# Every third image through the two-row form in both parts, in a convolution kernel with group normalisation

## The chip, the cores and the metric

One core of one Trainium2 chip. The metric is the device time of one execution in microseconds (us), the median of several runs. Each kernel was timed beside runs of the kernel before on the same chip.

Engines: PE is TensorE (PEld its weight loads), DVE is VectorE, ACT is the scalar engine, POOL is GpSimd, SP issues DMA. The timelines show the instructions of each of DVE, ACT and POOL in the order in which this program issues them (DVE of run e14 below has 30 in a row in that order, from 555.94 to 575.24 us).

## The reference, cut to what matters

```python
# x: (160, 128, 32, 32) fp32;  U: (5, 128*128*3*3)
v  = group_norm(x, 32 groups, eps=1e-5)       # over 4 channels x 32 x 32
s1 = (max(U) - min(U)) / 3;  v1 = s1 * floor(U / s1)
s2 = s1 / 5;                 v2 = s2 * floor((U - v1) / s2)
w  = (v1 + v2)                                # five sets of 3x3 weights, 128 -> 128
out = x + conv3x3(v, w[set of the image], pad=1)
```

Images are worked through set by set, 32 to a set. The weights of the next set are quantised while the present set is convolved.

## The kernel before: the parts that matter

fp16 matmuls are made accurate by splitting each normalised image z in two: `hi` (z in fp16) and `lo` (the rest). `hi` is convolved with all nine taps. `lo` goes through a **two-row form**: a pair of output rows is made from row differences `d` and from sums and differences `st` of row pairs, with combined weights, which needs fewer columns on PE. A sum `m` and the rest `eo` gather in PSUM, where PE's results lie until an engine fetches them; ACT moves `m` out, DVE forms the two rows of each pair and adds everything, and a DMA that accumulates adds the result to x in SBUF, from where it is stored.

```python
def conv(self, i, on_the_way):              # PE, image i
    ...                                     # m: 2 kinds x 3 columns, 512 wide, from st
    eo = ...
    for col in self.COLS:
        self.taps(i, (self.hi[i], 0), col, eo, False)     # 6 matmuls, 512 wide: hi, 3 taps x 2 halves
        ...                                               # 4 matmuls, 256 wide, from d
def leave(self, i):                         # ACT: m out of PSUM
def pairs(self, i):                         # DVE: two rows from each pair of m
def residual(self, i):                      # DVE: sum tile = pairs + eo; frees the PSUM tile eo
    self.sum[i] = self.sums.tile(...)       # pool "sums": 3 buffers
def accumulate(self, i):                    # POOL: DMA adds the sum tile to x
def store(self, i):                         # SP: store of a chunk of NB = 4 images

for i in range(self.imgs):                  # one round (cut)
    self.conv(i, on_the_way)
    self.normalise(i + 3)                   # ACT: z
    ...                                     # ACT: sum over image i + 13, if not by DVE
    self.leave(i)
    self.high_part(i + 3)                   # ACT: hi
    self.low_part(i + 2); self.combinations(i + 2)   # DVE
    self.residual(i - 1); self.pairs(i)              # DVE
    ...                                     # ACT: sum of squares; POOL: group means, deviations
    take(later, 2)                          # DVE: two steps of the next set's weights
    self.accumulate(i - 1); self.store(i - 2); ...   # loads
```

## Time and profile before

| | before |
|---|---|
| time | 1084.4 us (1083.8 to 1085.2) |
| busy | PE 97%, DVE 82%, ACT 71%, POOL 36% of 1082.9 us |
| chain that ended last | PE 94% |
| PE, one convolution | 6.42 us, 157 of them |

A line of groups reads: source line, engine, operation, result from operands, shape, count; then total busy us and mean ns of one; then the engine's idle time just before, and what ended most of it. In the timeline, a bracket holds the idle time before an instruction and what it waited for. The lines themselves are in the prediction below.

### The profile page before, as it was taken

The page shows a single profiled execution, that of the slowest core. Times are in us where ns is not written, and L with a number is a line of the kernel's source. Part 1 is how long each engine was busy: PE and PEld are TensorE (multiplying, and loading weights), DVE is VectorE, ACT ScalarE, POOL GpSimd, SP SyncE. Part 2 cuts the span into 40 slices and gives each one's busy share as a digit, 9 for nine tenths or more (in the row PEclk, how much of TensorE's full clock was granted, in tenths as well). Part 3 has the DMA queues.
Part 4 walks back from the last instruction along what each step waited for, and adds up shares of the span by engine and source line. Part 5 has one row for each costly group of instructions (what it writes and reads, how often), then busy time and mean ns, then how long its engine had stood idle before and what let it go on. Part 6 is the DMA issues. An engine that isn't in the chain of part 4 may idle for free.

```text
span 1082.9 us, 16003 instructions
## 1 busy us (share of the span) xinstructions
PE 1045.6 (97%) x5910; PEld 576.3 (53%) x5910; DVE 889.1 (82%) x1471; ACT 773.2 (71%) x1041; POOL 391.8 (36%) x738
## 2 busy tenths in 40 slices
PE   1899999999999999999999999999999999999997
PEld 0355555555555555555555555555555555555554
DVE  7998998877898988778898968798988777776774
ACT  4788886777768777767686877687777777677541
POOL 4634535332425343324435332334353313232210
PEclk9999999999999999999999999999999999999999
DMA  9518898989798889998897989798989898985764
GB/s 362 213 20 243 241 266 240 262 243 251 231 251 231 259 233 255 247 261 221 245 246 221 252 233 276 202 254 257 258 233 254 238 274 213 266 212 149 173 165 159
DMA packets 65462, 252.05 MB, mean 233 GB/s; under 512 B 3936, under 2 KB 3936, under 8 KB 65376
## 3 DMA queue, kind: packets, MB, share of 16 engines
q1 hardware_dynamic: 43344, 170.73, 42.2%
q0 software_dynamic: 22032, 80.23, 39.9%
q8 instruction: 48, 0.79, 0.3%
q14 instruction: 38, 0.31, 0.1%
HBM read 86.84 MB, written 83.89 MB: 158 GB/s over the span
## 4 chain that ended last, share of the span: by engine, by line
PE 94%; DVE 3%; ACT 1%; DMA 1%; issue 0%; POOL 0%; SPq 0%; DVEq 0%
PE eo L515 55%; PE eo L545 19%; PE m L545 19%; DMA u<-in_L_conv_U_dram 1%; PE m L515 1%; DVE ext L391 0%; DVE ext L392 0%; ACT z L468 0%; PE pt L428 0%; DVE tt L109 0%; PE pg L219 0%; DVE lo L481 0%; PE pg L204 0%; DVE k L113 0%; DVE tt L111 0%
## 5 line engine op out<-in xcount | busy, mean ns | idle before, releaser
L515 PE MATMUL eo<-hi,wt 128*128 128x512 f16 (+1 forms) x2862 | 684.7, 376 | 0.6 <-ACT wt L433 0.6
L515 PEld LDWEIGHTS <-wt 128*128 128x128 f16 x2934 | 287.7, 99 | 273.2 <-issue 2.3
L545 PEld LDWEIGHTS <-wt 128*128 128x128 f16 x2826 | 276.1, 98 | 194.9 <-issue 1.0
L545 PE MATMUL eo<-d,wt 128*128 128x256 f16 (+1 forms) x1884 | 283.3, 273 | 0.0
L573 ACT ACTIVATE mm<-m 128x1024 f16<-128x1024 f32 x157 | 159.8, 1018 | 158.0 <-PE m L545 157.9
L545 PE MATMUL m<-st,wt 128*128 128x512 f16 x942 | 229.3, 380 | 0.8 <-ACT mm L573 0.8
L468 ACT ACTIVATE z<-xt,shift,rstd 128x1024 f32<-128x1024 f32 x160 | 197.5, 1234 | 44.4 <-POOL shift L235 44.3
L481 DVE TENSOR_TENSOR lo<-z,hi 128x1024 f16<-128x1024 f32 x160 | 194.9, 1218 | 8.9 <-ACT hi L476 8.9
L602 DVE SCALAR_TENSOR_TENSOR sum<-pq,eo 128x1024 f32<-128x1024 f16 x153 | 185.5, 1213 | 17.5 <-PE eo L545 17.5
L582 DVE TENSOR_TENSOR pq<-mm 128x512 f16<-128x512 f16 x157 | 66.2, 422 | 135.2 <-ACT mm L573 134.0
L198 POOL TENSOR_SCALAR mv<-squares 128x1 f32<-128x1 f32 x121 | 63.5, 525 | 305.3 <-ACT junk L195 303.6
L615 POOL DMA_DIRECT2D xt<-sum x153 | 136.0, 891 | 85.3 <-DVE sum L602 69.5
L476 ACT CAST hi<-z 128x1024 f16<-128x1024 f32 x160 | 166.0, 1037 | 0.1
L195 ACT ACTIVATE junk<-xt,minus 128x1024 f16<-128x1024 f32 x121 | 139.1, 1150 | 2.6 <-POOL minus L188 1.4
L186 ACT ACTIVATE junk<-xt 128x1024 f16<-128x1024 f32 x121 | 126.4, 1045 | 12.1 <-DMA xt<-in_x_dram 11.9
L495 DVE TENSOR_TENSOR d<-lo 128x1024 f16<-128x1024 f16 x157 | 108.9, 694 | 5.4
L188 POOL TENSOR_SCALAR minus<-total 128x1 f32<-128x1 f32 x121 | 39.9, 329 | 97.2 <-ACT junk L186 96.5
L498 DVE TENSOR_TENSOR st<-lo 128x512 f16<-128x512 f16 x157 | 66.4, 423 | 0.0
L497 DVE TENSOR_TENSOR st<-lo 128x512 f16<-128x512 f16 x157 | 65.8, 419 | 0.0
L583 DVE TENSOR_TENSOR pq<-mm 128x512 f16<-128x512 f16 x157 | 65.4, 417 | 0.0
L179 DVE BATCH_NORM_STATS2 st<-xt 128x6 f32<-128x512 f32 x78 | 49.8, 679 | 0.0
L214 POOL TENSOR_TENSOR dv<-mv,ngm 128x8 f32<-128x8 f32 (+2 forms) x23 | 11.7, 509 | 89.6 <-ACT ngm L212 86.7
(96 smaller groups left out, 445.3 us busy)
## 6 DMA issues: line engine op xcount, KB each, us to landing
xt<-in_x_dram SPq DMA_DIRECT2D x39, 2048.0 KB, 14.0
out_dram<-xt SPq DMA_DIRECT2D x39, 2048.0 KB, 7.3
xt<-sum POOLq DMA_DIRECT2D x153, 512.0 KB, 8.2
u<-in_L_conv_U_dram SPq DMA_DIRECT2D x4, 576.0 KB, 8.1
xt<-in_x_dram SPq DMA_DIRECT2D x4, 512.0 KB, 10.5
out_dram<-xt SPq DMA_DIRECT2D x3, 512.0 KB, 3.1
u<-in_L_conv_U_dram SPq DMA_DIRECT2D x2, 288.0 KB, 3.0
out_dram<-xt SPq DMA_DIRECT2D x2, 256.0 KB, 3.5
```

The lines of the kernel that those rows point to most:

```text
L186: nc.scalar.activation(junk, image, ACTF.Copy, accum_out=total)
L195: nc.scalar.activation(junk, image, ACTF.Square, bias=self.minus[j], accum_out=squares)
L468: nc.scalar.activation(z, self.image(i), ACTF.Identity, bias=st.shift[:, j : j + 1], scale=st.rstd[:, j : j + 1],)
L476: self.nc.scalar.copy(hi.rearrange("p h w -> p (h w)"), self.z[i])
L481: self.nc.vector.tensor_sub(lo[:, 1 : self.H + 1, :].rearrange("p h w -> p (h w)"), self.z.pop(i), self.hi[i].rearrange("p h w -> p (h w)"),)
L495: nc.vector.tensor_sub(d, lo[:, 0:H, :], lo[:, 2 : H + 2, :])
L498: nc.vector.tensor_sub(st[:, 1], pairs[:, 1], pairs[:, 0])
L515: nc.tensor.matmul(target[:, h, r0 - h0 : r1 - h0, c0:c1], self.wts[n, col][:, k, :], tile[:, s0 : s0 + r1 - r0, c0 + dw : c1 + dw], start ...
L545: nc.tensor.matmul(target[:, :, c0:c1], self.wts[n, col][:, kind, :], source[:, :, c0 + dw : c1 + dw], start=start, stop=stop,)
L573: self.nc.scalar.mul(m, self.m.pop(i).rearrange("p a i w -> p a (i w)"), UP)
L602: nc.vector.scalar_tensor_tensor(self.sum[i], self.m.pop(i), 0.5 / UP, eo, ALU.mult, ALU.add)
L615: self.nc.gpsimd.dma_start(self.image(i), self.sum.pop(i), accum_op=ALU.add)
```

## The change

Every third image from image 14 on (48 of them) goes through the two-row form in **both** parts. For such an image DVE combines rows of x in fp32 (`v`), ACT rounds the combination to fp16 (`vh`), DVE makes the remainder (`vl`), and PE multiplies both. PE is rid of 18 wide taps, and runs the two-row form twice. Beside that, chunks become two images (11 buffers for 6 larger ones), all statistics from image 14 on move to ACT and are made one image earlier, and weights of later sets are loaded again when wanted. For the image after a combined one PE starts with `hi` and multiplies its `m` one column later (not in the cut below). A limit that guards the fast path is tightened for accuracy.

```diff
-NB = 4
+NB = 2
-LEAST, MOST = 2.0**-10, 0.06
+LEAST, MOST = 2.0**-10, 0.04
-    STAT_LEAD = 13
+    STAT_LEAD = 14
+    STEADY = 14
-        self.xpool = pool("x", 6)
+        self.xpool = pool("x", 11)
...
-        return i >= self.EARLY and (i % 4 == 0 or i == 10)
+        return self.EARLY <= i < self.STEADY and (i % 4 == 0 or i == 10)
...
+    def combined(self, i):
+        return self.STEADY <= i < self.imgs - LAST and i % 3 == 2
+    def combine(self, i):
+        v = self.v[i] = self.wide.tile([P, 2048], F32, tag="v", name=f"v{i}")
+        nc.gpsimd.tensor_scalar(v[:, :W], x[:, W : 2 * W], minus, -1.0, ALU.add, ALU.mult)
+        nc.gpsimd.tensor_scalar(v[:, last : H * W], ...)        # first and last row
+        nc.vector.tensor_sub(v[:, W:last], x[:, : last - W], x[:, 2 * W :])
+        nc.vector.scalar_tensor_tensor(s, pairs[:, 0], st.twice[:, j], pairs[:, 1], ALU.add, ALU.add)
+        nc.vector.tensor_sub(t, pairs[:, 1], pairs[:, 0])
+    def high_combined(self, i):
+        self.nc.scalar.mul(vh, self.v[i], st.rstd[:, j])
+    def low_combined(self, i):
+        self.nc.vector.scalar_tensor_tensor(vl, self.v[i], st.rstd[:, j], self.hi[i], ALU.mult, ALU.subtract)
...
     def pairs(self, i):
+        if self.combined(i):
+            pq = self.sums.tile([self.P, 1024], F32, tag="sum", name=f"sum{i}")
...
     def residual(self, i):
+        if self.combined(i):
+            nc.vector.tensor_add(self.sum[i], eo, self.sum[i])
...  # in the round of image i
+            if self.combined(i + 1):
+                self.low_combined(i + 1)
+            if self.combined(i + 2):
+                self.combine(i + 2)
...
+            if self.combined(i + 2):
+                self.high_combined(i + 2)
```

More of the change, by code (lines that the diff above doesn't have):

```diff
@@ L21 @@
 EPS = 1e-5
-NB = 4
+NB = 2
+LAST = 4
 LIFT = 2.0**14
-LEAST, MOST = 2.0**-10, 0.06
+LEAST, MOST = 2.0**-10, 0.04
 UP = 32.0
@@ L235, in scales @@
         nc.gpsimd.tensor_tensor(self.shift, self.ngm, self.rstd, ALU.mult)
+        self.twice = self.tile("twice", [self.nb])
+        nc.gpsimd.tensor_scalar_mul(self.twice, self.ngm, 2.0)
 def general_path(tc, keep, steps, x, u, out):
@@ L343, in __init__ @@
         self.wpool = pool("weights", 2)
-        self.xpool = pool("x", 6)
+        self.upool = pool("u", 1)
+        self.xpool = pool("x", 11)
         self.zpool = pool("z", 3)
-        self.parts = pool("parts", 5)
+        self.parts = pool("parts", 4)
         self.rows = pool("rows", 4)
+        self.wide = pool("wide", 1)
+        self.wide_parts = pool("wide_parts", 2)
         self.evac = pool("evac", 2)
@@ L369, in place, with space, load_set @@
         return divmod(i, self.per_set)
+    def space(self, name):
+        return self.xpool.tile([self.P, NB, 1024], F32, tag="xt", name=name)
+    def load_set(self, n):
+        self.us[n] = self.upool.tile([self.P, self.P, TAPS], F32, tag="u", name=f"u{n}")
+        self.nc.sync.dma_start(self.us[n], self.uv[n])
     def load(self, c, single=False):
-        xt = self.xpool.tile([self.P, NB, 1024], F32, tag="xt", name=f"xt{c}")
+        xt = self.space(f"xt{c}")
         self.chunks[c] = xt
@@ L477, in high_part, with column_of @@
         self.hi[i] = hi
+    def combined(self, i):
+        return self.STEADY <= i < self.imgs - LAST and i % 3 == 2
+    def column_of(self, i):
+        k = self.group_of[i]
+        j = i - self.groups[k].start
+        return self.stats[k], slice(j, j + 1)
+    def combine(self, i):
+        nc, P, H, W = self.nc, self.P, self.H, self.W
+        st, j = self.column_of(i)
+        v = self.v[i] = self.wide.tile([P, 2048], F32, tag="v", name=f"v{i}")
+        x = self.image(i)
+        minus, last = st.ngm[:, j], (H - 1) * W
+        nc.gpsimd.tensor_scalar(v[:, :W], x[:, W : 2 * W], minus, -1.0, ALU.add, ALU.mult)
+        nc.gpsimd.tensor_scalar(
+            v[:, last : H * W], x[:, last - W : last], minus, 1.0, ALU.add, ALU.mult
+        )
+        nc.vector.tensor_sub(v[:, W:last], x[:, : last - W], x[:, 2 * W :])
+        pairs = x.rearrange("p (i a w) -> p a i w", a=2, w=W)
+        s, t = (v[:, k : k + 512].rearrange("p (i w) -> p i w", w=W) for k in (1024, 1536))
+        nc.vector.scalar_tensor_tensor(
+            s, pairs[:, 0], st.twice[:, j], pairs[:, 1], ALU.add, ALU.add
+        )
+        nc.vector.tensor_sub(t, pairs[:, 1], pairs[:, 0])
+    def high_combined(self, i):
+        st, j = self.column_of(i)
+        vh = self.wide_parts.tile([self.P, 2048], MM, tag="vh", name=f"vh{i}")
+        self.nc.scalar.mul(vh, self.v[i], st.rstd[:, j])
+        self.hi[i] = vh
+    def low_combined(self, i):
+        st, j = self.column_of(i)
+        vl = self.rows.tile([self.P, 2048], MM, tag="rows", name=f"vl{i}")
+        self.nc.vector.scalar_tensor_tensor(
+            vl, self.v[i], st.rstd[:, j], self.hi[i], ALU.mult, ALU.subtract
+        )
+        self.v[i] = vl
     def low_part(self, i):
@@ L492, in combinations @@
         lo = self.los[i % len(self.los)]
-        d = self.rows.tile([P, H, W], MM, tag="d", name=f"d{i}")
-        st = self.rows.tile([P, 2, H // 2, W], MM, tag="st", name=f"st_{i}")
+        d, st = self.halves(self.rows.tile([P, 2048], MM, tag="rows", name=f"rows{i}"))
         nc.vector.tensor_sub(d, lo[:, 0:H, :], lo[:, 2 : H + 2, :])
@@ L499, in combinations, with halves @@
         self.v[i] = (d, st)
+    def halves(self, v):
+        return (
+            v[:, :1024].rearrange("p (h w) -> p h w", w=self.W),
+            v[:, 1024:].rearrange("p (a i w) -> p a i w", a=2, w=self.W),
+        )
     def taps(self, i, part, col, target, last):
@@ L539, in conv @@
         n, _ = self.place(i)
-        d, st = self.v.pop(i)
+        combined = self.combined(i)
+        if combined:
+            both = [self.halves(v) for v in (self.hi[i], self.v.pop(i))]
+        else:
+            both = [self.v.pop(i)]
+        late = self.combined(i - 1)
         def product(target, kind, source, col, start, stop):
@@ L551, in product, with sums_of_pairs @@
             )
-        m = self.m[i] = self.banks(self.ps_m, "m", i)
-        for a, kind in enumerate((self.SUM, self.DIFF)):
-            for col in self.COLS:
-                product(
-                    m[:, a], kind, st[:, a], col, col == self.COLS[0], col == self.COLS[-1]
-                )
+        def sums_of_pairs():
+            m = self.m[i] = self.banks(self.ps_m, "m", i)
+            for a, kind in enumerate((self.SUM, self.DIFF)):
+                for col in self.COLS:
+                    for _, st in both:
+                        product(
+                            m[:, a], kind, st[:, a], col,
+                            col == self.COLS[0] and st is both[0][1],
+                            col == self.COLS[-1] and st is both[-1][1],
+                        )
@@ L559, in conv @@
+        if not late:
+            sums_of_pairs()
         eo = self.eo[i] = self.banks(self.ps_eo, "eo", i)
         for col in self.COLS:
+            if late and col == self.COLS[1]:
+                sums_of_pairs()
             if col == self.COLS[-1]:
                 on_the_way()
-            self.taps(i, (self.hi[i], 0), col, eo, False)
+            if not combined:
+                self.taps(i, (self.hi[i], 0), col, eo, False)
             for a, kind in enumerate((0, self.MINUS_G2)):
-                for h in range(2):
-                    rows = slice(h * 16 + a, h * 16 + 16, 2)
-                    to = eo[:, h].rearrange("p (i a) w -> p i a w", a=2)[:, :, a, :]
-                    product(to, kind, d[:, rows, :], col, False, col == self.COLS[-1] and a == 1)
@@ L570, in leave @@
-    def leave(self, i):
-        m = self.evac.tile([self.P, 2, 512], MM, tag="mm", name=f"mm{i}")
-        self.nc.scalar.mul(m, self.m.pop(i).rearrange("p a i w -> p a (i w)"), UP)
+                for d, _ in both:
+                    for h in range(2):
+                        rows = slice(h * 16 + a, h * 16 + 16, 2)
+                        to = eo[:, h].rearrange("p (i a) w -> p i a w", a=2)[:, :, a, :]
+                        product(
+                            to, kind, d[:, rows, :], col,
+                            combined and col == self.COLS[0] and a == 0 and d is both[0][0],
+                            col == self.COLS[-1] and a == 1 and d is both[-1][0],
+                        )
@@ L574, in leave @@
+    def leave(self, i):
+        if self.combined(i):
+            m = self.wide.tile([self.P, 2, 512], F32, tag="m", name=f"mw{i}")
+            scale = 0.5
+        else:
+            m = self.evac.tile([self.P, 2, 512], MM, tag="mm", name=f"mm{i}")
+            scale = UP
+        self.nc.scalar.mul(m, self.m.pop(i).rearrange("p a i w -> p a (i w)"), scale)
         self.m[i] = m
@@ L579, in pairs @@
         m = self.m.pop(i).rearrange("p a (i w) -> p a i w", w=self.W)
-        pq = self.evac.tile([self.P, 1024], MM, tag="pq", name=f"pq{i}")
+        if self.combined(i):
+            pq = self.sums.tile([self.P, 1024], F32, tag="sum", name=f"sum{i}")
+        else:
+            pq = self.evac.tile([self.P, 1024], MM, tag="pq", name=f"pq{i}")
         rows = pq.rearrange("p (i a w) -> p i a w", a=2, w=self.W)
@@ L590, in by_hand @@
     def by_hand(self, i):
-        return i < self.FIRST or i >= self.imgs - NB
+        return i < self.FIRST or i >= self.imgs - LAST
     def residual(self, i):
@@ L599, in residual @@
         n, b = self.place(i)
+        if self.combined(i):
+            self.sum[i] = self.m.pop(i)
+            nc.vector.tensor_add(self.sum[i], eo, self.sum[i])
+            return
         if not self.by_hand(i):
@@ L609, in residual @@
             nc.vector.tensor_add(xj[:, h], eo[:, h], xj[:, h])
-            if i >= self.imgs - NB:
+            if i >= self.imgs - LAST:
                 nc.sync.dma_start(self.ov[n, :, b, h], xj[:, h])
@@ L617, in store @@
     def store(self, i):
-        if 0 <= i < self.imgs - NB and i % NB == NB - 1:
+        if 0 <= i < self.imgs - LAST and i % NB == NB - 1:
             n, b = self.place(i)
@@ L625, in run @@
         nc, P = self.nc, self.P
-        self.us = []
+        self.us = {}
         for n in range(N_SETS):
-            un = self.const.tile([P, P, TAPS], F32, tag=f"u{n}", name=f"u{n}")
+            if n == 0:
+                un = self.upool.tile([P, P, TAPS], F32, tag="u", name="u0")
+            else:
+                un = self.space(f"range{n}").rearrange("p j e -> p (j e)")[:, : P * TAPS]
+                un = un.rearrange("p (i k) -> p i k", k=TAPS)
             half = P // 2 if n == 0 else P
@@ L631, in run @@
                 nc.sync.dma_start(un[:, c : c + half], self.uv[n][:, c : c + half])
-            self.us.append(un)
-        self.load(0, single=True)
-        self.load(1)
-        self.load(2)
+            self.us[n] = un
+        for c in range(6):
+            self.load(c, single=c < 2)
         warm = self.const.tile([P, 1], F32, tag="warm", name="warm")
@@ L656, in run @@
         nc.vector.memset(self.ones, 1.0)
-        spread = self.over_partitions(self.weight_range(self.us), ident)
+        spread = self.over_partitions(self.weight_range(list(self.us.values())), ident)
         def take(steps, count):
@@ L731, in run @@
         self.steps.choose()
-        ready, middle, measured, loaded, later = [], [], self.EARLY, 3, None
+        ready, middle, measured, loaded, later = [], [], self.EARLY, 6, None
         for i in range(self.imgs):
@@ L758, in run @@
             measured += len(to_measure)
-            if self.FIRST < i + 3 < self.imgs:
-                self.normalise(i + 3)
+            parted = [
+                k for k in (i + 3, i + 4)
+                if self.FIRST < k < self.imgs and not self.combined(k)
+                and k - 3 - self.combined(k - 1) == i
+            ]
+            if self.combined(i + 1):
+                self.low_combined(i + 1)
+            if self.combined(i + 2):
+                self.combine(i + 2)
+            for k in parted:
+                self.normalise(k)
             for k in to_measure:
@@ L765, in run @@
                 self.leave(i)
-            if self.FIRST < i + 3 < self.imgs:
-                self.high_part(i + 3)
-            if self.FIRST < i + 2 < self.imgs:
-                self.low_part(i + 2)
-                self.combinations(i + 2)
+            for k in parted:
+                self.high_part(k)
+            if self.combined(i + 2):
+                self.high_combined(i + 2)
+            if i + 2 < self.STEADY:
+                if self.FIRST < i + 2:
+                    self.low_part(i + 2)
+                    self.combinations(i + 2)
             if i > self.FIRST:
@@ L774, in run @@
                 self.pairs(i)
+            if self.STEADY <= i + 2 < self.imgs and not self.combined(i + 2):
+                self.low_part(i + 2)
+                self.combinations(i + 2)
             for st in middle:
@@ L785, in run @@
                     ready.append(self.stats[group])
+            if b == self.per_set // 16 and n + 1 < N_SETS:
+                self.load_set(n + 1)
             if b == self.per_set // 8 and n + 1 < N_SETS:
```

## The prediction

> **What bounds the kernel now.** I read the page's totals and the chain that ended last first, then one image in the timeline, then the groups by form, then the waits, then DMA in slices of 1 us. Totals, clock and chain:
>
> ```profile
> PE 1045.6 (97%) x5910; PEld 576.3 (53%) x5910; DVE 889.1 (82%) x1471; ACT 773.2 (71%) x1041; POOL 391.8 (36%) x738
> ...
> PEclk9999999999999999999999999999999999999999
> ...
> PE 94%; DVE 3%; ACT 1%; DMA 1%; issue 0%; POOL 0%; SPq 0%; DVEq 0%
> ```
>
> The reader sees PE busy throughout, at full clock, and 94% of the chain is PE. The waits agree: PE's largest, 18.9 us, is one in the start-up, and in the 157 convolutions that follow it waits for others about 1 us. So this is a PE-bound kernel: the time is the start-up (the first such convolution starts near 66.7 us), 157 convolutions, and a short tail. What matters is what one convolution costs on PE. The timeline around 507 us, PE only:
>
> ```profile
> 506.91 1.46 PE L545 MATMUL m<-st,wt 128*128 128x512 f16 x6
> ...
> 508.21 1.43 PE L515 MATMUL eo<-hi,wt 128*128 128x512 f16 x6
> ...
> 509.48 0.60 PE L545 MATMUL eo<-d,wt 128*128 128x256 f16 x4
> 509.92 1.43 PE L515 MATMUL eo<-hi,wt 128*128 128x496 f16 x6
> ...
> 513.33 1.46 PE L545 MATMUL m<-st,wt 128*128 128x512 f16 x6
> ```
>
> Durations overlap (pipelined), so I take differences of starts: m to the next m is 6.42 us for 36 matmuls. Six 512-wide ones take 508.21-506.91 = 1.30 us (217 ns each), four 256-wide ones 509.92-509.48 = 0.44 us (110 ns each). A row of 31 costs like one of 32. Check: 6 + 18 x (full or 480) + 12 x 256 is 15,168 columns; at 2.4 per ns plus 36 x 2.5 ns that is 6.41 us.
>
> The other engines have room, but not much. The groups I use below:
>
> ```profile
> L468 ACT ACTIVATE z<-xt,shift,rstd 128x1024 f32<-128x1024 f32 x160 | 197.5, 1234 | 44.4 <-POOL shift L235 44.3
> L481 DVE TENSOR_TENSOR lo<-z,hi 128x1024 f16<-128x1024 f32 x160 | 194.9, 1218 | 8.9 <-ACT hi L476 8.9
> L602 DVE SCALAR_TENSOR_TENSOR sum<-pq,eo 128x1024 f32<-128x1024 f16 x153 | 185.5, 1213 | 17.5 <-PE eo L545 17.5
> L476 ACT CAST hi<-z 128x1024 f16<-128x1024 f32 x160 | 166.0, 1037 | 0.1
> L573 ACT ACTIVATE mm<-m 128x1024 f16<-128x1024 f32 x157 | 159.8, 1018 | 158.0 <-PE m L545 157.9
> L195 ACT ACTIVATE junk<-xt,minus 128x1024 f16<-128x1024 f32 x121 | 139.1, 1150 | 2.6 <-POOL minus L188 1.4
> L495 DVE TENSOR_TENSOR d<-lo 128x1024 f16<-128x1024 f16 x157 | 108.9, 694 | 5.4
> L582 DVE TENSOR_TENSOR pq<-mm 128x512 f16<-128x512 f16 x157 | 66.2, 422 | 135.2 <-ACT mm L573 134.0
> L179 DVE BATCH_NORM_STATS2 st<-xt 128x6 f32<-128x512 f32 x78 | 49.8, 679 | 0.0
> ```
>
> ACT sits 158 us waiting for PE and DVE 134 us waiting for ACT: slack to be spent. But in the busy times by stretch (us of each engine with its number of instructions, in the order PE, weight loads, DVE, ACT, POOL) DVE fills 24.1 of 26 us where the next set's weights are quantised, and 19.4 where not:
>
> ```profile
> 508.00:534.00 26.00, 26.00 (x151) 14.42 (x150) 24.09 (x42) 17.80 (x25) 9.15 (x13) 1.00 0.85 239
> ...
> 638.00:664.00 26.00, 26.00 (x148) 14.35 (x147) 19.39 (x32) 19.12 (x26) 8.84 (x20) 1.00 0.90 241
> ```
>
> **What the Trainium skill says.** (1) "TensorE: Matmul & The Clock Gate", section Back-to-back issue gap: warm, N/2.4 + 2.5 ns per matmul, so 216 ns at 512 and 109 at 256. The trace agrees (217, 110). The same section's sustained 131 ns at N=512 is not seen. A weight load takes 98 to 99 ns here, so it still hides behind a 256-wide matmul, barely. (2) "VectorE: DVE Perf Modes", section The perf-mode tier table: tensor_tensor runs 2x in 16 bits, 1x in fp32; the fp32 formula under its TRN2 errata section is (N+151)/0.96 ns. Agrees: 1024 fp32 give 1224 ns against 1218, and 1024 in 16 bits take 694. (3) "ScalarE: Activation LUTs", section What ACT_TABLE_LOAD costs: 186 ns + 0.833 N, plus 93 per pointer operand. Agrees: 1039 against 1037 (hi), 1225 against 1234 (z). (4) "SBUF — State Buffer", section Who interferes with whom: a VectorE op with two SBUF inputs contends with a GpSimd op that reads SBUF. The trace fits: the same one-element POOL op (L198) lasted 0.22 to 1.28 us in the timeline.
>
> **The change part by part.**
> *PE.* Images 14, 17, ..., 155 are combined: (155-14)/3 + 1 = 48. Each drops the 18 direct taps of the high part and does the two-row form twice: 12 x 512 + 24 x 256 = 12,288 columns, still 36 matmuls: 12,288/2.4 + 90 ns = 5.21 us. Saved: 6.41 - 5.21 = 1.20 us, x48 = **57.6 us**, all on the path. The instruction order confirms an unchanged PE instruction count. PE-bound floor: 1084.4 - 57.6 = 1026.8.
>
> *DVE.* Back-to-back an op costs its duration less some 0.09 us (starts in the timeline), and a dependent one its duration plus 0.03. A plain image: lo 1.25, d 0.60, st 0.67, sum 1.13, pq 0.67 = 4.3. A combined one, at fp32 1x: v over 960 columns 1.07, s and t (512 each, 0.60) 1.2, vl over 2048 (2199/0.96 = 2.29) 2.2, two fp32 pair ops 1.2, eo add 1.13 = 6.8. Of three images: 2 x 4.3 + 6.8 = 15.4, against PE's 2 x 6.41 + 5.21 = 18.03. So DVE fits without the weights (85%). With them, two steps per image, some 1.08 us (7.6 us per column over 7 images), it is 15.4 + 3.2 = 18.65: **over PE by 0.6 us per three images**. A column set takes about 21 images, four times: 7 x 0.6 = 4.3 us each. Putting the order of DVE's work beside PE's, the first to miss its time is the eo add of the image before a combined one (it frees a PSUM buffer), with 2 to 3 us of room. Lost: about 2 us x 4 = 8 us. The bn_stats that leave (36 images x 1.4 us) are already out of the 15.4.
>
> *ACT.* Per plain image with statistics z 1.14, hi 0.93, mm 0.92, sum 1.04, square 1.15 = 5.2; combined: vh over 2048 (186 + 93 + 1706 = 1.985) 1.9 in place of z and hi: 5.0. Three images: 15.4, 85% of 18.03. It fits, except at iterations 8 to 11, where two or three images are measured in each while 16, 20 and 24 are no longer VectorE's: some 7.4 us of work against 6.4, after stretches where it was already at 25.1 of 26 us. Lost once: 3 us.
>
> *POOL.* Two 32-column rows per combined image and three small ops for each of 36 images: under 1 us per image on an engine at 36%; only delay.
>
> *DMA.* Bytes nearly as before (a second read of four weight sets, 2.4 MB). But a load now follows the store of the pair before it at once, issued three images before use. Slices of 1 us show the DMA engines full for long stretches (last columns: clock, DMA share, GB/s), and the page's table of issues gives the landing times:
>
> ```profile
> 347.00:348.00 1.00, 1.00 (x7) 0.54 (x6) 1.00 (x3) 1.00 (x2) 0.00 (x0) 1.00 1.06 201
> ...
> xt<-in_x_dram SPq DMA_DIRECT2D x39, 2048.0 KB, 14.0
> out_dram<-xt SPq DMA_DIRECT2D x39, 2048.0 KB, 7.3
> xt<-sum POOLq DMA_DIRECT2D x153, 512.0 KB, 8.2
> ```
>
> Mean share over 92 to 950 us is some 0.88; at 18.03 us per three images instead of 19.26 that becomes 0.94. The loop: accumulate, landing in 8.2 us (row of DMA issues), then store and load, the load landing in perhaps 9 to 10 (2 MB took 14.0), is 18 to 19 us. The accumulate goes out at the end of one iteration, and ACT first reads the loaded pair at the start of the fourth after it, so three whole iterations, 18.0 us, lie between, plus some 1 us of z ahead of that read and ACT's idle time. It just fits; I choose 3 us lost.
>
> Sum: 1026.8 + 8 + 3 + 3 = 1041.
>
> **Rivals.** (a) *DVE becomes the bound throughout.* For it: 24.1 of 26 us already; waits for vh or for POOL's two rows would stop DVE in order. Against: 15.4 of 18.03 outside the weights. If DVE ran 10% worse than my sum it would bind in the weight stretches by 2.4 us per three images: 28 x 2.4 = 67 us less slack, and the time is near 1080. (b) *Loads become the wait.* For: the share of 0.94 and the loop above. Against: queues shorten as soon as PE slows, and ACT has 2.6 us idle in three images. If each of some 70 loads came 0.5 us too late, 35 us: about 1073 in place of my 1041 (1041 - 3 + 35). (c) *Nothing binds*, buffers absorb the weight stretches: 1028 to 1032.
>
> **Range and chances.** Predicted 1041 us. From (c) with a small start-up loss to a mix of (a) and (b): 1029 to 1062. Faster by over 2% means under 1062.8: 0.88, since it takes 36 us of new waits to miss it. Within 2%: 0.10. Slower by over 2%: 0.02.
>
> **What would show it.** PE busy near 990 us and 94 to 96% of a shorter span; m to m about 5.2 us in a combined image, 6.4 otherwise; 48 vl ops of 2.29 us, vh of 1.99; DVE total about 930 us, ACT about 830. PE waits of a few us in all for DVE's eo add or vl, bunched at weight stretches (b between 4 and 24 of each set), and for ACT near image 10. ACT's sums waiting for loads under 30 us in all. Wrong would be: 256-wide matmuls, now 24 in a row, slower than 110 ns because weight loads no longer hide; DVE waits for POOL's rows; or sums waiting for loads each pair.

## More of the kernel before

The rounds of experiments ran on different chips; the kernel before took 1084.0 to 1084.6 us in each of them.

## The result, and the profile after

The changed kernel took **1148.21 us** (1146.53 to 1153.46, 4 runs) against 1084.12 us beside it: 1.0598 times as long (95% interval 1.0561 to 1.0635). A ratio here is the mean time of one kernel's fast runs over that of the other's in the same rounds, so not quite the ratio of the medians quoted. The page's totals, clock by slice, and the chain that ended last, of the changed kernel:

```profile
PE 1023.7 (89%) x5910; PEld 582.4 (51%) x5910; DVE 962.7 (84%) x1363; ACT 841.9 (74%) x1137; POOL 596.4 (52%) x965
...
PEclk9999999999998999999989999999999999999999
...
ACT 21%; DMA 18%; POOL 18%; PE 17%; DVE 13%; issue 12%; SPq 0%; POOLq 0%; DVEq 0%; ACTq 0%
```

PE is no longer full (89%), and no engine carries the chain: from PE 94% it went to six shares of 12 to 21%. I took that for the sign of a **loop of waits**: work is passed round among the engines, and it is the time of one turn that counts, not how busy anyone is. The new instructions cost what was expected (groups by form, changed kernel; the second number after the bar is the mean ns of one):

```profile
L536 DVE SCALAR_TENSOR_TENSOR vl<-v,rstd,vh 128x2048 f16<-128x2048 f32 x48 | 112.7, 2349 | 11.6 <-ACT vh L530 11.6
L530 ACT ACTIVATE vh<-v,rstd 128x2048 f16<-128x2048 f32 x48 | 96.1, 2002 | 148.6 <-DVE v L525 100.3 <-POOL v L516 30.4 <-POOL mv L190 17.9
```

It is the last column that is new: ACT stood 148.6 us in front of `vh`, 3.1 us each time on average. The waits (engine, line, waited for; us in total, times, longest) show what stands behind it:

```profile
ACT vh L530 <- DVE v L525: 100.3, 24, 7.8
...
DVE sum L679 <- DMA xt<-sum: 60.3, 18, 6.1
PE eo L583 <- DVE sum L699: 55.9, 25, 3.5
```

DVE waits for the accumulating DMA before it may write the pair rows of a combined image. ACT then waits for DVE, and PE for DVE's add of the finished PSUM tile. The timeline of the changed kernel shows such a turn (start, us):

```profile
669.52 0.71 DVE L679 TENSOR_TENSOR sum<-mw 128x512 f32<-128x512 f32 x1 [4.05 <-DMA xt<-sum]
...
675.02 0.68 DVE L525 TENSOR_TENSOR v<-xt 128x512 f32<-128x512 f32 x1
675.62 1.22 DVE L699 TENSOR_TENSOR sum<-eo,sum 128x1024 f32<-128x1024 f32 x1
675.80 2.00 ACT L530 ACTIVATE vh<-v,rstd 128x2048 f16<-128x2048 f32 x1 [5.73 <-DVE v L525]
...
676.90 2.07 PE L583 MATMUL eo<-hi,wt 128*128 128x512 f16 x6 [2.33 <-DVE sum L699]
...
679.61 2.10 PE L583 MATMUL eo<-hi,wt 128*128 128x496 f16 x6
...
681.54 0.60 PE L619 MATMUL eo<-rows,wt 128*128 128x248 f16 x4
```

The pair rows of a combined image are fp32 and are written into a sum buffer, of which there are three, and this happens one round earlier than a plain image takes its sum buffer. So DVE waits 4.05 us for an older accumulate to land, then works through its list up to `v`; `vh` comes 5.73 us late, and PE stands for 2.33 us. PE then pays a second time. The granted clock in the two stretches after the gap is the last figure but two of these lines (the first two are the stretch and its length, then the engines as before):

```profile
676.90:679.60 2.70, 2.70 (x10) 1.32 (x10) 2.37 (x3) 2.70 (x5) 1.65 (x1) 0.62 0.79 311
679.60:681.50 1.90, 1.90 (x8) 0.79 (x6) 1.72 (x2) 1.90 (x4) 1.64 (x5) 0.64 0.02 6
```

These are means: in shorter slices of the same trace the clock is 1.00 up to 677.4 us, 0.50 from 677.6 to 680, and 1.00 again from 681. The six matmuls and the four that follow took 679.61 - 676.90 = 2.71 us in place of 1.71, and the next six 1.93 in place of 1.27, 1.66 us lost on top of the gap. Over the run the mean clock fell to 0.975 from 0.998.

### The profile page after: what moved, and what is told of

Read it like the earlier page. It is cut to its first block, busy times and chain, and to the rows that moved or that the text cites. A ratio compares the mean times of both kernels' runs of the same rounds, so it can differ in the third digit from the quotient of the medians.

```text
span 1145.2 us, 16411 instructions
## 1 busy us (share of the span) xinstructions
PE 1023.7 (89%) x5910; PEld 582.4 (51%) x5910; DVE 962.7 (84%) x1363; ACT 841.9 (74%) x1137; POOL 596.4 (52%) x965
## 4 chain that ended last, share of the span: by engine, by line
ACT 21%; DMA 18%; POOL 18%; PE 17%; DVE 13%; issue 12%; SPq 0%; POOLq 0%; DVEq 0%; ACTq 0%
DMA xt<-sum 15%; PE eo L583 8%; ACT junk L187 4%; ACT vh L530 4%; PE m L619 4%; ACT junk L196 4%; PE eo L619 4%; ACT z L486 4%; DMA xt<-in_x_dram 3%; POOL mv L199 3%; POOL v L516 3%; POOL rstd L229 2%; POOL xt L716 2%; DVE lo L543 2%; ACT hi L494 2%
## 5 line engine op out<-in xcount | busy, mean ns | idle before, releaser
L583 PE MATMUL eo<-hi,wt 128*128 128x496 f16 (+3 forms) x1998 | 497.1, 387 | 57.4 <-DVE sum L699 55.9
L530 ACT ACTIVATE vh<-v,rstd 128x2048 f16<-128x2048 f32 x48 | 96.1, 2002 | 148.6 <-DVE v L525 100.3
L619 PE MATMUL eo<-rows,wt 128*128 128x248 f16 (+1 forms) x1308 | 201.6, 278 | 0.0
L619 PE MATMUL m<-rows,wt 128*128 128x496 f16 (+1 forms) x654 | 159.6, 380 | 18.6 <-ACT mm L667 7.1
L486 ACT ACTIVATE z<-xt,shift,rstd 128x1024 f32<-128x1024 f32 x112 | 137.9, 1231 | 25.5 <-POOL shift L236 25.5
L536 DVE SCALAR_TENSOR_TENSOR vl<-v,rstd,vh 128x2048 f16<-128x2048 f32 x48 | 112.7, 2349 | 11.6 <-ACT vh L530 11.6
L679 DVE TENSOR_TENSOR sum<-mw 128x512 f32<-128x512 f32 x48 | 33.5, 697 | 99.7 <-DMA xt<-sum 60.3
L619 PE MATMUL m<-vh,wt 128*128 128x496 f16 (+1 forms) x288 | 110.6, 384 | 6.6 <-ACT mm L667 6.6
L494 ACT CAST hi<-z 128x1024 f16<-128x1024 f32 x112 | 116.0, 1036 | 0.1
L619 PE MATMUL m<-vl,wt 128*128 128x496 f16 (+1 forms) x288 | 110.6, 384 | 0.0
L619 PE MATMUL eo<-vl,wt 128*128 128x248 f16 (+1 forms) x576 | 110.2, 273 | 0.0
L619 PE MATMUL eo<-vh,wt 128*128 128x248 f16 (+1 forms) x576 | 110.1, 273 | 0.0
```

Source lines behind the costliest of these rows:

```text
L486: nc.scalar.activation(z, self.image(i), ACTF.Identity, bias=st.shift[:, j : j + 1], scale=st.rstd[:, j : j + 1],)
L494: self.nc.scalar.copy(hi.rearrange("p h w -> p (h w)"), self.z[i])
L530: self.nc.scalar.mul(vh, self.v[i], st.rstd[:, j])
L536: self.nc.vector.scalar_tensor_tensor(vl, self.v[i], st.rstd[:, j], self.hi[i], ALU.mult, ALU.subtract)
L583: nc.tensor.matmul(target[:, h, r0 - h0 : r1 - h0, c0:c1], self.wts[n, col][:, k, :], tile[:, s0 : s0 + r1 - r0, c0 + dw : c1 + dw], start ...
L619: nc.tensor.matmul(target[:, :, c0:c1], self.wts[n, col][:, kind, :], source[:, :, c0 + dw : c1 + dw], start=start, stop=stop,)
```

## The experiments

The changed kernel is called **after** below. I started from three theories: S, the wait for sum buffers; P, GpSimd's two rows of each combination, behind GpSimd's other work in order; L, late loads. Two more came later: V, VectorE's own sum where weights are made; and the ring.

### First four: buffers, rows, and the change without combining

e1 is after with five sum buffers. e2 is after with the first and last row of each combination on VectorE. e3 has both. e4 has everything but the combining.

```diff
-        self.sums = pool("sums", 3)                                   # e1, e3
+        self.sums = pool("sums", 5)
-        nc.gpsimd.tensor_scalar(v[:, :W], ...)                        # e2, e3, and the last row
+        nc.vector.tensor_scalar(v[:, :W], ...)
-        return self.STEADY <= i < self.imgs - LAST and i % 3 == 2     # e4
+        return False
```

Expected of e1:

> The changed kernel with five sum buffers in place of three. Theory S (a combined image takes its sum buffer one step earlier than a plain one, so VectorE waits for the accumulate three images back to land, 60 us of waits in 18 places, and scalar engine, GpSimd and TensorE follow): that wait goes to under 5 us and the time falls by 40 to 90 us, to 1060-1105. Rival P (GpSimd's share of the combination, two rows behind its other work in order, is what makes the loop long): the wait goes, others take its place, time stays over 1125. Rival L (loads of two images arrive late): time stays over 1125 and the scalar engine's wait for loads grows over its 33 us.

Expected of e2:

> The changed kernel with three sum buffers, but the first and last row of each combination on VectorE in place of GpSimd (two ops of about 0.2 us more for each of 48 images). Theory S: the wait for accumulates stays at 40 us or more, time within 20 us of 1148. Rival P: the 48 us that the scalar engine waits for GpSimd before vh go, time falls by 40 us or more. Rival L: no change.

Expected of e3:

> Both edits. Theory S: no more than 15 us below the run with five sum buffers alone. Rival P: 30 us or more below that run. If neither loop matters any more, the time should be near my sum of 1041 (1030 to 1060).

Expected of e4:

> The changed kernel with no image combined: loads of two, later statistics all on the scalar engine, the earlier statistics lead and eleven x buffers stay. Theory S and rival P: the rest of the change costs nothing much, TensorE is the bound again at 6.41 us per image, time 1080 to 1095. Rival L: the loss is in the loads or statistics, time 1110 or more.

| | median us | over before |
|---|---|---|
| after | 1148.2 | 1.060 |
| e1, five sum buffers | 1105.7 | 1.019 |
| e2, rows on VectorE | 1151.0 | 1.061 |
| e3, both | 1104.9 | 1.019 |
| e4, no image combined | 1090.5 | 1.006 |

The wait for sum buffers is worth 42 us, as S said, and is gone from the waits of e1. P alone is refuted here: moving the rows changed nothing (e2, and e3 against e1). e4 says that the rest of the change costs 6.5 us, so the bulk is in the combining. But e3 is still 64 us over my 1041, so S was not the whole.

### Next four: loads, weights, every fourth image, another order

All have five sum buffers and issue loads two images earlier (e5). e6 makes no weights for sets 1 to 4 and uses those of set 0, so its result is wrong. e7 combines every fourth image. e8 lets DVE free the PSUM tile before it combines the next image, which looked like the cure for PE's wait for that add.

```diff
-    LOAD_LEAD = 17                                                    # e5 to e8
+    LOAD_LEAD = 19
-                later = (s for col in self.COLS for s in self.make_column(n + 1, col))   # e6
+                for col in self.COLS:
+                    self.wts[n + 1, col] = self.wts[0, col]
-... and i % 3 == 2                                                     # e7
+... and i % 4 == 2
-            if self.combined(i + 2):                                  # e8: from the head of the round
-                self.combine(i + 2)
             ...
-            if self.combined(i + 2):
-                self.high_combined(i + 2)
             ...
             if i > self.FIRST:
                 self.residual(i - 1)
+            if self.combined(i + 2):
+                self.combine(i + 2)
+                self.high_combined(i + 2)
```

Expected of e5:

> Five sum buffers, and loads issued two images earlier (the load waits for the store of the same buffer instead of for the next pair's accumulate). Theory L2 (with the sum buffers cured, the next latency loop is accumulate, store, load, statistics; the chain of the five-buffer runs has 9.4 + 11.2 us of it in a row): scalar engine's waits for loads in the body go to near 0 and the time falls by 15 to 40 us from 1105. Rival V (VectorE is the bound in the weight stretches and its order holds the PSUM buffer back): falls by under 10 us.

Expected of e6:

> As e5, and the weights of sets 1 to 4 are not made (set 0's are used again, so the result is wrong on purpose): VectorE is rid of two steps, 1.08 us, per image in four stretches of 21 images, 91 us in all. Theory V: 25 to 45 us below e5. Rival: under 10 us below e5, as TensorE or latency loops hold the time.

Expected of e7:

> As e5, with every fourth image combined in place of every third: 36 images, TensorE's floor rises by 12 x 1.20 = 14.4 us, VectorE's work falls by 12 x 2.5 = 30 us. Theory V: at least 10 us below e5, and 15 us or more below 1084 (about 1055 to 1070). Rival (latency loops per combined image): between e5 minus 10 and e5.

Expected of e8:

> As e5, with VectorE adding the finished PSUM tile (which frees it) before it combines the image after next, not after. Theory V's order part: TensorE's wait for that add (23 to 30 us in 22 to 26 places with five buffers) goes to under 5 us, and time falls by 10 to 25 us from e5. Rival: the combination is later now, vh and vl with it, and the time stays within 8 us of e5.

| | median us | over before |
|---|---|---|
| e5, loads earlier | 1100.8 | 1.015 |
| e6, and no weights | 1058.5 | 0.976 |
| e7, and every fourth | 1067.8 | 0.985 |
| e8, e5 in the other order | 1152.0 | 1.062 |

Earlier loads took ACT's waits for them down to the start-up's 11.7 us, but were worth only 5 us against e1 (by the ratios 4): L is a small term. e6 is 42 us below e5, so V is real. (The edit takes 89.5 us of work from DVE, but also 6.4 us from ACT, 36 instructions from GpSimd and 36 matmuls from PE; I put the gain down to DVE.) e7 gives up 14.4 us of PE's gain and still ends 33 us below e5. e8 was a plain miss, and the most telling run: expected faster, it lost 51 us. PE's wait for the adds did go (26.2 us to 3.0). But `combine` now stood behind the add, ACT waited 125.0 us for `v` (49.1 in e5), and PE 72.8 us for ACT to empty `m` (20.0 in e5). So I took the moment at which DVE delivers `v` to ACT to matter more than when it frees PSUM.

### Four more: what is left without weights, the start-up, and where to combine

e9 is e6 with the rows on VectorE. e10 is e7 with the rows on VectorE and the statistics of images 16, 20 and 24 on VectorE again. e11 is e4 with that last edit alone. e12 is e10 with as many combined images (36) placed otherwise.

```diff
-        return self.EARLY <= i < self.STEADY and (i % 4 == 0 or i == 10)    # e10, e11, e12
+        return self.EARLY <= i < 26 and (i % 4 == 0 or i == 10)
+        while i < self.imgs - LAST:                                         # e12
+            self.chosen.add(i)
+            n, b = self.place(i)
+            i += 5 if 4 <= b <= 26 and n + 1 < N_SETS else 3
```

Expected of e9:

> Five sum buffers, loads two images earlier, no weights made for sets 1 to 4 (wrong result on purpose), and the two rows of a combination on VectorE, not GpSimd. With every wait found so far taken away and VectorE's weight work too. Theory G (what is left above the floor in the run without weights is GpSimd's 45 late rows, 94 us of waits before vh): time falls by 10 to 25 us from 1058.5, to 1033-1048. Rival (the scalar engine's own work and start-up hold it): stays at 1053 or more.

Expected of e10:

> Every fourth image, five sum buffers, loads two images earlier, rows on VectorE, and the statistics of images 16, 20 and 24 on VectorE again. If GpSimd's rows and the start-up each still cost: 1052 to 1062, 5 to 15 us below the 1067.8 of the run with every fourth image. If VectorE in the weight stretches is what is left, the rows only move work to it: 1060 to 1066.

Expected of e11:

> No image combined, and the statistics of images 16, 20 and 24 on VectorE again. If the 6.5 us by which the run without combining is over the kernel before are the scalar engine's catch-up near image 10: within 2 us of before (1083 to 1086.5). If they come from the loads of two: still 1088 or more.

Expected of e12:

> As e10 and again 36 images combined, but every fifth where weights are made and every third elsewhere. Theory V (VectorE is over TensorE only in the weight stretches: by my count 24.7 to 24.4 us per four images, 30.1 to 30.9 per five): 4 to 12 us below e10, 1045 to 1055. Rival (only the number of combined images counts): within 3 us of e10.

| | median us | over before |
|---|---|---|
| e9, e6 with rows on VectorE | 1055.6 | 0.974 |
| e10, every fourth, all cures | 1045.1 | 0.964 |
| e11, e4 with three statistics back | 1083.5 | 0.999 |
| e12, every fifth or third | 1046.4 | 0.966 |

e11 settles the 6.5 us of e4. They were ACT's catch-up near image 10 (it measures images that VectorE no longer takes); in e4's timeline of PE five convolutions in a row begin with a wait for ACT, of which this one, and in e11's none does:

```profile
106.32 1.46 PE L619 MATMUL m<-rows,wt 128*128 128x512 f16 x6 [1.24 <-ACT mm L667]
```

e10 did better than the 1052 to 1062 expected, 22.7 us below e7. Some 7 us of that are the start-up (e4 to e11). The other 16 would be GpSimd's rows, for which ACT had waited 80.6 us in e7; no run moves the rows alone at every fourth image, so that is by difference only. It also bounds what e2 and e3 say: the rows cost nothing there, in a turn that something else held. e12 missed: the same count placed otherwise gained nothing over e10, as its rival said. And e9 missed: GpSimd's rows were not what was left, since the 94 us that ACT had waited for them turned into 92 us of waits for DVE. With buffers cured and VectorE at 84%, why did e9 stay 29 us above the floor of 1026.8, of which the start-up explains 7? The chain of e9 in order of time gives the answer. In this stretch it leaves PE and goes round two engines (start, us; ACT `junk` lines are the sum and the squares of an image's statistics; of a `vh`, which lasts 2.00 us, the chain lists the first 0.03):

```profile
299.87 0.03 ACT vh L530
...
301.78 1.22 ACT junk L196 x2
303.00 1.13 ACT z L486
304.14 1.04 ACT junk L187 x2
305.18 0.91 ACT mm L667
...
310.33 0.92 ACT mw L667
...
311.27 0.69 DVE sum L679
...
312.57 1.15 DVE lo L543
...
317.12 0.61 DVE v L525
...
317.76 2.00 ACT vh L530
```

This is **the ring**. From `vh` to `vh`: ACT works through two images in order until it moves `m` of the combined image out (`mw`, 11.38 us). DVE then forms the pair rows, the low part of a plain image and the next combination, also in order (6.46 us). Then comes the next `vh`. That is 317.76 - 299.87 = 17.89 us, against 18.03 us that PE needs for three images. Nothing may be added to it. When the statistics of a group of images are finished inside it, ACT waits for them, 2.82 us at 328.99 us, and the next turn took 20.9 us. Two weight steps, a wait for a sum buffer or a late row would lengthen it in the same way.

### The ring taken apart

Issuing each combination one image earlier takes the combination out of the ring, and leaves every engine's work as it is. e13 is the control: every third image with all cures. e14 is e13 with that edit, e15 the same without weights (result wrong), and e16 is **after itself with this edit alone**.

```diff
-            if self.combined(i + 2):
-                self.combine(i + 2)
+            if self.combined(i + 3):
+                self.combine(i + 3)
```

Expected of e13:

> Control: every third image combined, five sum buffers, loads two images earlier, rows on VectorE, statistics of images 16, 20, 24 on VectorE, true weights. By the single effects so far (1100.8 with two of these, about 7 us for the statistics, a few for the rows): 1085 to 1096.

Expected of e14:

> The control with each combination issued one image earlier on VectorE (same work on every engine). Ring theory: the ring through scalar engine and VectorE no longer holds, only VectorE's sum in the weight stretches does, 19.3 against 18.03 us per three images, 28 times, some 25 to 36 us over a floor of 1027: 20 to 40 us below the control. Rival (VectorE's total work is the bound already, or the PSUM buffer is freed later now): within 8 us of the control.

Expected of e15:

> The run without weights and with all cures (1055.6), the statistics of 16, 20, 24 on VectorE (about 7 us, so 1048.6), and combinations one image earlier; wrong result on purpose. Ring theory: near the floor of 1026.8, 1029 to 1040. Rival: 1045 or more.

Expected of e16:

> The changed kernel itself, three sum buffers, loads, rows on GpSimd and statistics as they are, with only the combinations one image earlier. If the wait for a sum buffer costs through the ring (it stands ahead of the combination that vh waits for): 30 us or more below 1148. If it costs by itself, holding VectorE's later work: within 15 us of 1148.

The last column is the mean time from `vh` to `vh`, from the first and last start of its 48 instances divided by 47; PE alone would need 18.03.

| | median us | over before | `vh` to `vh`, us |
|---|---|---|---|
| after | 1148.2 | 1.060 | 20.6 |
| e1, five sum buffers | 1105.7 | 1.019 | 19.7 |
| e9, all cures but the start-up's, no weights | 1055.6 | 0.974 | 18.7 |
| e13, every third, all cures | 1088.3 | 1.004 | 19.5 |
| e14, and combined one image earlier | 1075.3 | 0.992 | 19.2 |
| e15, and no weights | 1036.8 | 0.956 | 18.4 |
| e16, after, combined one image earlier | 1088.6 | 1.003 | 19.4 |

One moved call, e16, gives back 60 of the 64 us, with three sum buffers, late loads and rows on GpSimd all left as they were. ACT no longer waits for `v` before any `vh`. So the ring is shown. The wait for sum buffers fell with it, from 60.3 us in 18 places to 8.0 in 7, though there are still three. That fits a buffer wait that cost its 42 us by lengthening the ring; e16 does not hold that wait and take away the ring alone, so the two are not separated further. With everything else cured the edit is worth 13 us (e13 to e14), less than the 20 I had put at least. e14 to e15, the weights, is 38.5 us: theory V, now without the ring (and with the same side effects as in e6). e14's timeline of DVE in a weight stretch shows no gap from one `vl` to the next but one:

```profile
536.04 2.35 DVE L536 SCALAR_TENSOR_TENSOR vl<-v,rstd,vh 128x2048 f16<-128x2048 f32 x1
...
555.94 2.35 DVE L536 SCALAR_TENSOR_TENSOR vl<-v,rstd,vh 128x2048 f16<-128x2048 f32 x1
...
575.24 2.35 DVE L536 SCALAR_TENSOR_TENSOR vl<-v,rstd,vh 128x2048 f16<-128x2048 f32 x1
```

The second turn is 575.24 - 555.94 = 19.30 us of work without a wait. VectorE is 1.3 us over PE per three images there, not 0.6. Without weights and ring, e15 is PE-bound again and 10 us above the floor:

```profile
PE 989.1 (96%) x5874; PEld 574.4 (55%) x5874; DVE 887.3 (86%) x1300; ACT 827.3 (80%) x1101; POOL 549.3 (53%) x824
...
PE 58%; ACT 17%; DVE 10%; POOL 7%; issue 6%; DMA 1%; SPq 0%; DVEq 0%; POOLq 0%; ACTq 0%
```

### The last two

e17 is e10 without the ring. e18 combines every fourth image where weights are made and every third elsewhere, 40 images, without the ring.

```diff
-            if self.combined(i + 2):                                  # e17 (from e10), e18 (from e12)
-                self.combine(i + 2)
+            if self.combined(i + 3):
+                self.combine(i + 3)
-            i += 5 if 4 <= b <= 26 and n + 1 < N_SETS else 3          # e18
+            i += 4 if 4 <= b <= 26 and n + 1 < N_SETS else 3
```

Expected of e17:

> The best run so far (every fourth image, all cures, 1045.1) with the combinations one image earlier. With a round of four images the ring is about 23 us (17.9 and 5.2 for one more image on the scalar engine) against TensorE's 24.4, so it should no longer matter: within 4 us of 1045. If the ring still costs there: 1040 or less (the floor for 36 images is 1084.4 - 43.2 = 1041).

Expected of e18:

> 40 images: every fourth where weights are made, every third elsewhere, combinations one image earlier. Floor 1084.4 - 48 = 1036.4. If only VectorE's sum in the weight stretches is left: 1036 to 1044, a few us below e17. If rounds of three still lose outside the stretches too: 1044 or more.

e17 took 1045.15 us (0.964 of before) and e18 1046.3 (0.965). With four images to a turn the ring has slack and removing it changes nothing, as expected. e18's four more images brought nothing: it missed its 1036 to 1044 and fell in the other branch, 1044 or more. Its trace shows where they went: PE is busy 4.0 us less than in e17, but waits 6.3 us for DVE's adds, against 1.2 there. The best version is e10 (or e17): **1045.1 us, correct, 3.6% faster than before**, and PE-bound again:

```profile
PE 1005.5 (96%) x5910; PEld 576.4 (55%) x5910; DVE 943.4 (90%) x1444; ACT 837.1 (80%) x1137; POOL 528.2 (51%) x860
...
PE 64%; DVE 22%; ACT 7%; POOL 3%; issue 3%; DMA 1%; SPq 0%; DVEq 0%; POOLq 0%; ACTq 0%
```

## Why the prediction was wrong, point by point

It said 1041, with 0.02 for slower by over 2%. It was 1148.

1. **What bounds the kernel before, and PE's saving: right.** A combined image's convolution takes 5.22 us in the changed kernel (its first matmul at 642.40, the next image's at 647.62), predicted 5.21. The rate feared for 24 narrow matmuls in a row held: the 24 from 644.99 to 647.62 took 110 ns each. PE's busy time was foreseen near 990 us and is 989.1 in e15, which has 36 matmuls fewer. No run contradicts the floor of 1026.8: e15 came to 1036.8, and e10 to 4 us above its own of 1041. One reading was off, without consequence: the first two-row convolution starts at 59.16 us; the one at 66.70 is the second.
2. **The costs of the new instructions: right**, within 3% (`vl` 2.35 against 2.29 us, `vh` 2.00 against 1.985), and so were the busy totals of ACT (842 against 830). DVE's 963 against 930 was 4% off.
3. **The step that failed is the one after: "DVE fits without the weights", ACT's "It fits", and so "Lost: about 2 us x 4".** Each engine's work per three images was compared with PE's, one engine at a time: 15.4 of 18.03 for DVE, 15.4 for ACT. But the combined image makes ACT wait for DVE (`vh` for `v`) and DVE wait for ACT (pair rows for `mw`) in every turn, in order on both. The two engines' pieces add up to 17.9 us in one ring. At 85% each, together they left 0.1 us. Rival (a) did speak of DVE stopping in order for `vh`, but for a DVE that is full; none of the three counted the way round. e16 shows it: the same work, one call earlier, 60 us back.
4. **Sum buffers: not looked at.** The diff moves the allocation of a sum buffer from `residual` to `pairs`, one round earlier, with three buffers kept. The table of issues gave 8.2 us for an accumulate to land, longer than a round of 6.4. A combined image takes the buffer only about one round after the accumulate that must free it has gone out. That the wait would appear could have been worked out; it is worth 42 us (e1).
5. **DVE in the weight stretches: right in kind, too small.** Foreseen 0.6 us per three images and 8 us in all after slack; measured 1.3 us (19.30 against 18.03) and 38.5 us (e14 to e15). Of the 0.65 us missing in the sum, 0.29 are the two rows that e14 put on DVE; by the starts in that turn the rest is 0.15 on the combined image's own operations, 0.12 on the weight steps and 0.1 on the two plain images. 28 turns of 1.3 us are 36 us, near the 38.5, so the 2 to 3 us of room foreseen do not show.
6. **ACT at the start, 3 us: 7.0 measured** (e4 to e11). **Loads, 3 us: about 5** (e1 to e5). Right in kind.
7. **Not foreseen: the clock.** PE's busy time rose to 1023.7 us in the changed kernel, 35 us more than in e15. The timeline above shows one case in full (gap of 2.33 us, then 1.66 us lost on slow matmuls). In slices of 1 us the trace has, from 60 us on, 14 stretches at a clock of 0.50, each at a gap of 2.2 us or more in PE's work; twelve are worth 1.7 us at full clock and two 3.4, 27 us in all. Of the rest of the 35, up to 4 us are the 36 matmuls that e15 lacks; what is left is not accounted for.

Open in part: the 10 us between e15 and the floor. PE's own waits there show where nearly all of them are lost:

```profile
PE eo L583 <- DVE sum L703: 9.2, 12, 1.7
```

Six of the twelve, 0.81 us each, come 20.6 us after ACT has waited 3.9 us for the statistics' shift (33.1 us in 11 places in all). So I take those waits for the cause of the largest part, but no run removed them. Open too is why DVE's adds come late in e18.

## What to carry to other kernels

When a change gives two in-order engines something to pass back and forth in every turn, add up the whole way round, engine by engine and wait by wait, and compare that sum with the bound engine's time for the same turn; here the busy shares of 84% and 79% did not show it. A chain that was 94% one engine and came out in six shares of 12 to 21% was such a ring here, and issuing one link of it earlier gave back more (60 us) than two more buffers did (42). And when a diff moves an allocation, count the time from a buffer's last use to its new first use.

## What the Trainium skill lacked or had wrong

- "TensorE: Matmul & The Clock Gate", section Why this matters for your kernels, warns of PE-idle gaps of more than about 3 us. Here a gap of 2.33 us, with one of 0.53 us shortly before, was enough: the granted clock fell to 0.50 for over 3 us, and 1.66 us were lost on top of the gap. It was not always enough: of the ten gaps of 2.2 to 2.4 us in this trace from 60 us on five came with such a stretch and five did not; all nine longer ones did, and none of those under 2 us.
- "SBUF — State Buffer", section Who interferes with whom, says that a VectorE op with two SBUF inputs contends with GpSimd's reads, and that the shared ports are an exclusive lock, but has no measured time for a short GpSimd op beside long VectorE ones. The same GpSimd op on 128x32 elements (L516) took 0.29 to 2.81 us here, median 1.23, beside VectorE ops of up to 2.35 us; the same two rows took 0.23 us each on VectorE. That fits the lock; that the contention is the cause was not tested apart.
- No page has the check: the time round a ring of in-order engines (17.89 us here, of 18.03 available, with ACT at 79% and DVE at 84%).
- "VectorE: DVE Perf Modes": its fp32 formula (N+151)/0.96 held for tensor_tensor (960 columns: 1157 ns, measured 1157). For scalar_tensor_tensor with a per-partition scalar from SBUF, which the formula does not name, it was 58 to 63 ns short (2048: 2291 against 2349; 512: 691 against 754).
